# Attention layers on one core: the output projection as seven half products over two halves of an image, with its weight sums kept in DRAM, one pool of half tiles, and residuals added on GpSimd

## The chip, the cores and the metric

The kernel runs on one core of a Trainium2 chip. The core has five engines that run their own instruction streams and wait for each other through semaphores: TensorE (PE in the profile, its weight loads PEld), VectorE (DVE), ScalarE (ACT), GpSimd (POOL) and SyncE (SP), whose queue here issues nearly all DMAs. The metric is the time on the device in microseconds (us); lower is better. Everything is computed in float32.

## The reference

Two layers over four images of 32 x 32 positions and 768 channels. Each layer normalises its input in 32 groups of channels, does self-attention with 12 heads of 64 channels and a position bias in both directions, projects, and adds its input:

```python
qkv = x @ Wqkv
...
rel_h = jnp.einsum('bhwc,hkc->bhwk', r_q, Rh)
rel_w = jnp.einsum('bhwc,wkc->bhwk', r_q, Rw)
...
scores = scale * jnp.einsum('bqc,bkc->bqk', q, k) + bias
attn = jax.nn.softmax(scores, axis=-1)
out = jnp.einsum('bqk,bkc->bqc', attn, v)
...
return out @ Wproj + bproj
...
x = x + _L0_conv_ref(_gn(x), ...)
x = x + _L1_conv_ref(_gn(x), ...)
```

The second layer has other weights, biases on q, k and v, and another scale of the bias. An image has S = 1024 positions, so the output projection is a product of 768 x 768 weights with 768 x 1024 values for each of eight layer-images.

## The kernel before, in words

The eight layer-images ("images" from here, 0 to 7; 4 to 7 are the second layer) are worked one after the other. An image has six pairs of heads; a pair has eight units, each of 128 query positions for both heads. So there are 48 pairs and 384 units, and the loop over units (`for at, (g, n) in enumerate(units)`) writes out by hand the order of all engines' work. Channels lie on partitions, 128 at a time, as six chunks c, and the 1024 positions are two halves of 512.

In the iteration of a unit, GpSimd makes the bias tiles `sc` of the unit two ahead (`biases`, L535: two tensors of 128 x 1024), TensorE makes the scores of the next unit (L549), VectorE adds them to the bias and finds the row extremes (L561), ScalarE takes exponentials (L565), VectorE the reciprocal (L573), ScalarE or, in two of eight units, GpSimd divides one of the two heads (L579, L577). VectorE then transposes the present unit's tiles in blocks of 32 into `tb` (L585); SP stores `tb` to DRAM (`td`, L587) and one to three units later reads it back in the transposed order (`pt`, L596). At the end of units 6 and 2 `weigh` multiplies the values with the probabilities of the first and the second half of a pair (L614). `sc` has six buffers (three units), `tb` two, `td` five, `pt` two (a quarter of a pair each).

Between these come pieces of matmuls for other pairs. The projections of q, k and v (`products`, `values`) already work on sums of weights and of halves of x, seven products instead of eight. A function `crossed` (L356) runs a group of 12 matmuls of 64 contraction rows in two halves of six; the second half uses the other rows for each output. A `Crossed` object issues one half at each call; a table `same` says in which unit which half goes: the output groups O0 and O1 go in unit 5 (O0), unit 7 (O0, O1) and unit 0 of the next pair ("O1 previous"), between a first q group (G0) and a first v group (V0).

The output projection itself is done directly: for each of six output chunks o, three input chunks at a time (p = 0 in pairs 3 to 5 of the same image, p = 1 in pairs 0 to 2 of the next), `project_out_two` gives both halves. `put_result` adds the residual and the bias on VectorE (L711), SP stores this partial sum to DRAM and reads it back for p = 1 (L713), whose result is stored. In the last image the second part has no next image: groups of single matmuls (L693, contraction over 128 rows) are held in `todo` and taken in the last pair, some in each unit as `shares` says, the rest after the loop.

The next image's x is loaded in halves. Images 1 to 3 load one half early in the pair 0 for its statistics, and then again for use; GpSimd makes sums of halves in pairs 4 and 5. The group norm of the next image (`norm`) gathers means through DRAM in units 1 to 7 of pair 3 with four small DMAs, and ScalarE applies it in pair 4.

What waits for a free buffer waits on the engine or the queue that writes it first; SP's queue keeps its order, so what stands behind a waiting DMA waits too.

## Time and profile before

| | |
|---|---|
| median of three runs | 3295.09 us (3294.67 to 3298.21) |
| the profiled execution | 3297.59 us, its span 3295.9 |
| granted TensorE clock | 0.999 |
| TensorE matmul, weight loads | 99%, 57% of the span |
| VectorE, ScalarE, GpSimd | 78%, 61%, 74% |
| DMA | 1047.33 MB, mean 318 GB/s |
| output groups oo, L356 | x2112 records, mean 589 ns |
| bias tiles, L535 | x768, mean 2555 ns |

A matmul instruction of float32 leaves two records, so 2112 are 88 groups of 12. Matmuls on the two row halves overlap, so a record's mean is longer than what it adds to the engine's time; in the chain of work, which lists pieces in order of time with their start, length and engine, a piece's length is what it adds. In the table of stretches each engine's busy time is followed by its number of instructions; after the engines come the granted clock, the busy share of the 16 DMA engines and the rate in GB/s. Square brackets behind an instruction are the idle time before it and who ended it.

### The profile page before, as it was taken

What the parts mean: (1) busy time and instruction counts of PE and PEld (TensorE: products, weight loads), DVE (VectorE), ACT (ScalarE), POOL (GpSimd) and SP (SyncE); (2) the same over time, 40 slices, a digit from 0 to 9 for tenths busy, and PEclk for the clock granted to TensorE, in tenths of its full rate; (3) what the DMA queues carried; (4) which work ended last, traced back from release to release, by engine and by line L of the source; (5) the groups of instructions that cost most, each with busy time, mean ns of one, the idle gap of its engine ahead of it and who ended that gap; (6) DMA issues with size and microseconds to landing.
All of it is one profiled execution on the core that took longest, in us unless ns stands there. A gap on an engine that the chain in (4) does not pass through costs nothing.

```text
span 3295.9 us, 64321 instructions
## 1 busy us (share of the span) xinstructions
PE 3269.2 (99%) x25076; PEld 1880.4 (57%) x25076; DVE 2559.5 (78%) x4087; ACT 2002.4 (61%) x3004; POOL 2437.8 (74%) x1249
## 2 busy tenths in 40 slices
PE   8999999999999999999999999999999999999998
PEld 5565555555565555555565555655555555655554
DVE  7887778877787777787778877777777777777775
ACT  5676656666556665656656666555756566565653
POOL 7877967679677786777867778677786777777762
PEclk9999999999999999999999999999999999999999
DMA  5999899999999998999889999898998989898887
GB/s 182 331 337 328 319 330 329 320 332 319 327 337 315 333 323 304 338 322 329 316 313 335 317 330 319 314 330 315 337 320 312 324 315 341 312 319 310 318 287 272
DMA packets 395152, 1047.33 MB, mean 318 GB/s; under 512 B 34656, under 2 KB 60768, under 8 KB 345696
## 3 DMA queue, kind: packets, MB, share of 16 engines
q1 hardware_dynamic: 379296, 1015.79, 87.2%
q10 hardware_dynamic: 15552, 27.43, 2.2%
q8 instruction: 198, 3.24, 0.4%
q14 instruction: 106, 0.87, 0.1%
HBM read 568.00 MB, written 475.09 MB: 316 GB/s over the span
## 4 chain that ended last, share of the span: by engine, by line
PE 96%; DMA 2%; DVE 1%; issue 0%; ACT 0%; POOL 0%; SPq 0%; DVEq 0%; POOLq 0%; ACTq 0%
PE pj L356 22%; PE av L614 20%; PE s L549 20%; PE oo L356 14%; PE pv L356 11%; PE pj L384 4%; PE tp L487 2%; PE pv L441 2%; DMA td<-tb 1%; PE o L693 1%; DVE tb L585 1%; DMA xn<-in_x 0%; DMA pt<-td 0%; DVE sc L561 0%; DVE s L325 0%
## 5 line engine op out<-in xcount | busy, mean ns | idle before, releaser
L535 POOL TENSOR_TENSOR sc<-rel 128x1024 f32<-128x1024 f32 x768 | 1937.9, 2555 | 426.9 <-DVE tb L585 406.8
L561 DVE CUSTOM_DVE_ANT_0 sc<-s,sc 128x1024 f32<-128x1024 f32 x768 | 911.3, 1223 | 363.9 <-PE s L549 316.2
L579 ACT ACTIVATE sc<-sc,sm 128x1024 f32<-128x1024 f32 x674 | 743.5, 1144 | 613.1 <-DVE sm L573 461.0
L565 ACT ACTIVATE sc<-sc,sm 128x1024 f32<-128x1024 f32 x768 | 878.7, 1146 | 360.4 <-DVE sm L561 357.8
L585 DVE STREAM_TRANSPOSE tb<-sc 128x1024 f32<-128x1024 f32 x768 | 908.5, 1224 | 13.5 <-DMA td<-tb 12.7
L549 PE MATMUL s<-k,q 64*128 64x512 f32 x3072 | 738.1, 596 | 1.9 <-DVE sm L561 1.4
L614 PE MATMUL av<-pt,v 128*64 128x256 f32 x6144 | 686.4, 381 | 5.6 <-DMA pt<-td 4.0
L614 PEld LDWEIGHTS av<-pt,v 128*64 128x64 f32 x6144 | 435.1, 137 | 286.4 <-issue 40.5
L356 PE MATMUL oo<-attn,wo 64*128 64x512 f32 x2112 | 475.3, 589 | 0.0
L549 PEld LDWEIGHTS s<-k,q 64*128 64x128 f32 x3072 | 284.4, 187 | 300.3 <-issue 267.4
L577 POOL TENSOR_SCALAR sc<-sc,sm 128x1024 f32<-128x1024 f32 x94 | 105.7, 1124 | 351.4 <-DVE sm L573 351.4
L356 PEld LDWEIGHTS oo<-attn,wo 64*128 64x128 f32 x2112 | 200.9, 187 | 228.0 <-issue 227.0
L356 PEld LDWEIGHTS pv<-wv,xn 64*128 64x128 f32 x4608 | 270.8, 188 | 35.0 <-issue 25.6
L356 PE MATMUL pv<-wv,xn 64*128 64x128 f32 x4608 | 273.2, 272 | 0.6 <-DVE wv L345 0.6
L356 PE MATMUL pj<-xn,wa 64*128 64x512 f32 x1152 | 264.3, 590 | 1.6 <-DVE xn L253 1.0
L356 PE MATMUL pj<-xn,w 64*128 64x512 f32 x1152 | 263.2, 589 | 0.0
L356 PE MATMUL pj<-s,wc 64*128 64x512 f32 x576 | 262.6, 589 | 0.0
L356 PE MATMUL pj<-s,w 64*128 64x512 f32 x576 | 262.6, 589 | 0.0
L356 PEld LDWEIGHTS pj<-xn,w 64*128 64x128 f32 x1152 | 111.7, 187 | 135.5 <-issue 133.8
L356 PEld LDWEIGHTS pj<-xn,wa 64*128 64x128 f32 x1152 | 111.6, 187 | 135.6 <-issue 123.6
L458 DVE TENSOR_TENSOR v<-pv,v 128x512 f32<-128x512 f32 x216 | 140.2, 686 | 57.4 <-ACT v L460 42.4
L510 ACT COPY rel<-raw 32x256 f32<-32x256 f32 x384 | 154.9, 403 | 3.6
(102 smaller groups left out, 2656.4 us busy)
## 6 DMA issues: line engine op xcount, KB each, us to landing
td<-tb SPq DMA_DIRECT2D x384, 1024.0 KB, 5.4
pt<-td SPq DMA_DIRECT2D x382, 1024.0 KB, 8.6
tdr<-t ACTq DMA_DIRECT2D x96, 256.0 KB, 5.4
part<-res SPq DMA_DIRECT2D x84, 256.0 KB, 4.2
res<-part SPq DMA_DIRECT2D x84, 256.0 KB, 4.7
wa<-in_wqk SPq DMA_DIRECT2D x48, 384.0 KB, 3.9
wc<-in_wqk SPq DMA_DIRECT2D x48, 384.0 KB, 5.3
wv<-in_wv SPq DMA_DIRECT2D x24, 768.0 KB, 11.2
```

The source lines that it names most:

```text
L356: nc.tensor.matmul(to, lhsT=w, rhs=x, start=at == half == 0, stop=at == 0 and half == 1)
L384: nc.tensor.matmul(t[:, h, :], lhsT=w[rows, c, :], rhs=x[c][rows, :], start=(c == 0), stop=(c == NB - 1),)
L458: add = lambda to, x, y: nc.vector.tensor_tensor(to, x, y, ALU.add)
L510: nc.scalar.copy(rel[rows], raw[rows, :, :, WIDE - 1 - HW - y : WIDE - 1 - y])
L535: nc.gpsimd.tensor_tensor(sc.rearrange("p (a k) (u l) -> p a (k u) l", a=4, l=8), rel[:, h, m, :].unsqueeze(1).unsqueeze(3).to_broadcast(s ...
L549: nc.tensor.matmul(ps[h][:, cols], lhsT=q[rows, n * P : (n + 1) * P], rhs=k[rows, cols], start=True, stop=True,)
L561: nc.vector.tensor_tensor_reduce(out=sc, in0=ps[h], in1=sc, scale=-scale, scalar=BIG, op0=ALU.add, op1=ALU.min, accum_out=st[:, 0, h : h + 1],
L565: nc.scalar.activation(sc, sc, AF.Exp, bias=st[:, 0, h : h + 1], scale=-1.0, accum_out=st[:, 1, h : h + 1],)
L577: nc.gpsimd.tensor_scalar(sc, sc, st[:, 2, h : h + 1], 1.0, ALU.mult, ALU.mult)
L579: nc.scalar.mul(sc, sc, st[:, 2, h : h + 1])
L585: nc.vector.transpose(tb[:, :, h, :], sc_of[g, n, h])
L614: nc.tensor.matmul(av[rows, at * 2 * P : (at + 1) * 2 * P], lhsT=v_of[g][:, k, rows], rhs=pt_of[g, quarter].rearrange("p n r k h i -> p (n ...
```

## The change

The output projection of images 0 to 6 is now done from all six chunks at once, as seven half products. Write the weights as four blocks of three chunks by three and the attention as two chunk groups by two position halves. For each o in 0 to 2 (chunks o and o + 3 of the output) there are four groups: a, b and c are crossed groups of two products each, d an uncrossed group of six matmuls with one product. The groups go in pairs 4 and 5 (a) of the image and 0 to 3 (b, c, d) of the next. Parts of the result are held in half tiles (`kept_x`, `kept_y`) and finished on VectorE.

- The sums of weight blocks are made once, by GpSimd in image 0 (units 8 to 28: `combined`, four loads, four subtractions and four stores for each of six layer and o combinations), kept in DRAM and loaded like the weights.
- The sums of attention halves are made by GpSimd (`out_sums`, 12 per image, in pairs 4, 5, and 0 and 2 of the next).
- The residual is loaded a unit after a result is there, added by GpSimd in the unit after that, and stored in the next (`complete`). Partial sums no longer go through DRAM.
- `xn`, attention, residuals and partial results are half tiles of one pool with 35 buffers; v has three buffers instead of four, output weights four instead of two.
- x of the next image is loaded whole at the start of pair 4 (six halves in unit 0, three each in units 1 and 2); for images 1 to 3 twelve halves are loaded in pairs 0 to 3 for the statistics alone.
- Group norm works on chip: VectorE transposes blocks of 32, sums over groups, squares on GpSimd, in units 6 and 7 of pair 3 and unit 0 of pair 4.
- In the last image only two output groups are done early instead of four; eight pieces of p = 0 instead of four are in `todo`, and `shares` grows from 18 to 33 matmuls.

```diff
+UNITS = 35
...
-    xpool = ctx.enter_context(tc.tile_pool(name="x", bufs=3 * NC))
-    apool = ctx.enter_context(tc.tile_pool(name="attn", bufs=6))
+    upool = ctx.enter_context(tc.tile_pool(name="unit", bufs=UNITS))
-    vpool = ctx.enter_context(tc.tile_pool(name="v", bufs=4))
+    vpool = ctx.enter_context(tc.tile_pool(name="v", bufs=3))
-    iopool = ctx.enter_context(tc.tile_pool(name="io", bufs=4))
...
+        def spread(to, x):
+            total = work[:, : HW // n]
+            nc.vector.tensor_reduce(total, by_group(x), mybir.AxisListType.X, ALU.add)
+            nc.vector.tensor_scalar(
+                by_group(to), total.unsqueeze(2).to_broadcast([P, HW // n, n]), 1.0 / n, None, ALU.mult
+            )
+        def group_means():
+            nc.vector.tensor_copy(w0[:, :2], means[:, im, :])
+            nc.vector.transpose(w1, w0)
+            spread(w0, w1)
...
+    def combined(l, o, stage, held={}):
+        if stage == 0:
+            tables[l, o] = dram.tile([4, P, NB * P], FP, tag=f"tw{l}_{o}", name=f"tw_{l}_{o}")
+            held[l, o] = [unit(f"t{k}_{l}_{o}")[:, : NB * P] for k in range(4)]
+            for k, t in enumerate(held[l, o]):
+                nc.sync.dma_start(
+                    out=t, in_=a[f"wo{l}"][o + k % 2 * NB][:, k // 2 * NB * P : (k // 2 + 1) * NB * P]
+                )
+            return
+        b11, b12, b21, b22 = held[l, o]
+        sub = lambda to, x, y: nc.gpsimd.tensor_tensor(to, x, y, ALU.subtract)
+        if stage == 1:
+            sub(b11, b12, b11)
+            sub(b12, b22, b12)
+        elif stage == 2:
+            sub(b22, b22, b11)
+            sub(b21, b21, b22)
+        else:
+            for k, t in enumerate((b11, b22, b12, b21)):
+                nc.sync.dma_start(out=tables[l, o][k], in_=t)
...
+    def out_product(im, kind, o):
...
+        if kind == "d":
+            for c in range(NB):
+                for h, rows in enumerate(ROWS):
+                    nc.tensor.matmul(
+                        t[:, h, :], lhsT=ws[0][rows, c, :], rhs=half(1, 0)[c][rows],
+                        start=(c == 0), stop=(c == NB - 1),
+                    )
+        else:
+            xs = {
+                "a": lambda: (half(0, 0), [s3_of[im, c] for c in range(NB)]),
+                "b": lambda: (half(1, 0), half(0, 0)),
+                "c": lambda: (half(0, 1), half(1, 1)),
+            }[kind]()
+            yield from crossed(t, range(NB), lambda t, c, h, rows: (
+                t[:, h, :], ws[h][rows, c, :], xs[h][c][rows]
+            ))
...
+        if kind == "a":
+            kept_x[o], kept_y[o] = unit(f"ox_{im}_{o}"), unit(f"oy_{im}_{o}")
+            nc.scalar.copy(kept_x[o], t0)
+            add(kept_y[o], t1, kept_x[o])
+        elif kind == "b":
+            x, y, r = kept_x[o], kept_y[o], unit(f"or_{im}_{o}_0")
+            with_bias(r, t0, x, o)
+            add(x, t1, x)
+            add(y, t1, y)
+            complete(im, o, 0, r)
...
+    def complete(im, o, i, r, delay=1):
+        l, b = images[im]
+        def load():
+            res = unit(f"res_{im}_{o}_{i}")
+            load_half(res, l, b, o, i)
+            at_sums.setdefault(here[0] + 1, []).append(lambda: add(res))
+        def add(res):
+            nc.gpsimd.tensor_tensor(res, res, r, ALU.add)
+            at_start.setdefault(here[0] + 1, []).append(lambda: store(res))
...
+    out_plan = {
+        0: ("b0", "b1", None), 1: ("b2", "c0", None), 2: ("c1", "d0", "d1"), 3: ("c2", "d2", ""),
+        4: ("a0", "", ""), 5: ("a1", "a2", None),
+    }
...
+    streams = [(0, n) for n in range(6)] + [(1, 3), (1, 4), (2, 4), (2, 5), (3, 3), (3, 4)]
...
+    out_sum_steps = {
+        (4, 0): (0, 3, 0), (4, 1): (0, 3, 1), (4, 2): (0, 3, 2), (5, 2): (0, 1, 0), (5, 4): (0, 1, 1),
+        (0, 3): (1, 1, 2), (0, 1): (1, 2, 0), (0, 2): (1, 2, 1), (0, 4): (1, 2, 2),
+    }
+    combining = {}
+    for k in range(LAYERS * NB):
+        for stage in range(4):
+            combining.setdefault(NT + 4 * k + stage + (stage > 0), []).append((k // NB, k % NB, stage))
...
-                    todo = put_out(im, 0, range(8, 12)) + put_out(im, 1, range(12))
+                    todo = put_out(0, range(4, 12)) + put_out(1, range(12))
-            shares = [0, 3, 0, 4, 4, 3, 0, 4]
+            shares = [3, 6, 0, 6, 6, 6, 0, 6]
```

## The prediction

> **What bounds the kernel now.** I read the engine totals first, then the chain that ended last, then stretches of about one pair of heads each, and last the queues of the two runners-up, DMA and GpSimd.
>
> ```profile
> PE 3269.2 (99%) x25076; PEld 1880.4 (57%) x25076; DVE 2559.5 (78%) x4087; ACT 2002.4 (61%) x3004; POOL 2437.8 (74%) x1249
> ...
> PE 96%; DMA 2%; DVE 1%; issue 0%; ACT 0%; POOL 0%; SPq 0%; DVEq 0%; POOLq 0%; ACTq 0%
> ```
>
> TensorE is busy 99% of the span and is 96% of the chain; every other engine has at least a fifth of the time free. The stretches below are pairs 1, 2, 3 and 4 of the first image, then pairs 3, 4 and 5 of the fourth, roughly, then the end of the last pair.
>
> ```profile
> core 0: us, PE busy (x) PEld busy (x) DVE busy (x) ACT busy (x) POOL busy (x), PEclk, DMA share, GB/s
> 93.00:154.00 61.00, 58.52 (x456) 34.90 (x456) 49.91 (x80) 39.57 (x60) 50.45 (x26) 0.97 0.94 344
> 154.00:214.00 60.00, 59.42 (x504) 36.26 (x502) 51.96 (x86) 39.42 (x60) 46.56 (x22) 1.00 0.91 318
> 214.00:273.00 59.00, 58.56 (x466) 33.88 (x462) 50.14 (x84) 42.47 (x63) 50.45 (x26) 1.00 0.91 329
> 273.00:342.00 69.00, 69.00 (x550) 41.12 (x549) 53.83 (x84) 46.55 (x70) 51.44 (x26) 1.00 0.94 336
> 1427.00:1493.00 66.00, 66.00 (x500) 37.41 (x498) 53.23 (x92) 42.24 (x63) 48.80 (x26) 1.00 0.91 318
> 1493.00:1562.00 69.00, 69.00 (x550) 40.26 (x548) 53.48 (x86) 46.59 (x71) 51.78 (x27) 1.00 0.95 336
> 1562.00:1628.00 66.00, 66.00 (x500) 37.37 (x498) 49.75 (x78) 41.47 (x62) 60.33 (x35) 1.00 0.90 319
> 3202.00:3257.00 55.00, 49.71 (x234) 23.39 (x232) 43.21 (x65) 33.72 (x45) 30.21 (x12) 1.00 0.93 324
> ```
>
> In the middle TensorE has no gap at all, so every matmul taken out there should shorten the run until something else is late. The next thing is near: DMA is at 0.90 to 0.95. Where it was full, it moved this much:
>
> ```profile
> 280.00:300.00 20.00, 20.00 (x143) 11.05 (x144) 14.14 (x23) 12.16 (x20) 13.59 (x7) 1.00 1.00 352
> 320.00:340.00 20.00, 20.00 (x114) 9.78 (x113) 17.57 (x30) 14.80 (x22) 16.29 (x9) 1.00 0.98 356
> ```
>
> So I take 354 GB/s as its ceiling. From the chain in order of time come the prices on TensorE: one half of a crossed group (12 records) is 2.58, a group without crossing (pj L384, six matmuls) also 2.58, and the single matmuls at the end 21.45/24 = 0.89 each.
>
> ```profile
> 258.73 2.58 PE pj L384 x12
> ...
> 268.17 2.58 PE oo L356 x12
> ...
> 3257.19 21.45 PE o L693 x48
> ```
>
> GpSimd's slack in pair 4 of the fourth image is what it waits before its three divisions, after which it must do the sums of the next image:
>
> ```profile
> 1528.41 1.12 POOL L577 TENSOR_SCALAR sc<-sc,sm 128x1024 f32<-128x1024 f32 x1 [6.25 <-DVE sm L573]
> ...
> 1545.36 1.12 POOL L577 TENSOR_SCALAR sc<-sc,sm 128x1024 f32<-128x1024 f32 x1 [3.72 <-DVE sm L573]
> ...
> 1597.95 1.12 POOL L577 TENSOR_SCALAR sc<-sc,sm 128x1024 f32<-128x1024 f32 x1 [5.12 <-DVE sm L573]
> ```
>
> [...] VectorE's own sum of two SBUF tiles took 1214 ns (s, L325), the same size with one PSUM operand 686 (v, L458). All new VectorE additions take one operand from PSUM[...].
>
> **The change, part by part.**
> *Seven half products.* Images 0 to 6 had 12 crossed groups each of 2 x 2.58 = 5.16. Now they have nine and three uncrossed ones of 2.58: 3 x 2.58 = 7.7 less per image, lying in pair 4 unit 0, pair 4 unit 7 and pair 5 unit 0. But the groups also move. Image 0's pairs 3 to 5 held six groups and now hold three (a0, a1, a2 in pairs 4 and 5): -15.5. Images 1 to 6: -7.7 x 6 = -46.4. Image 7's stretch had ten groups (six for image 6, four of its own) and gets six crossed, three uncrossed and two of its own: -2.6; the two groups it no longer does early become 12 single matmuls in the last pair, 12 x 0.89 = +10.7. Together -53.8 of TensorE time.
>
> *Bytes.* Summed over the program's DMAs, 1043.1 MB becomes 1025.4: the partial sums (22.0 written, 22.0 read) and group norm's small round trips go; three more weight loads per output chunk pair and the table come (24 loads and 24 stores of 0.197 for the table). But the table is made in image 0, units 8 to 28, and streams and residuals are spread anew. In pairs 1, 2, 3 of image 0 the bytes go from 19.4, 19.4, 18.9 to 22.0, 22.8, 23.6 MB: 68.4 MB, at 354 GB/s 193 us. TensorE's work there is 58.5 + 59.4 + (58.6 - 2.6 for the half group that goes) = 174. DMA becomes the bound for these three pairs and is 19 us short. Part of it is taken up by the distance between a probability tile's store and its use (its read is issued nearly three units before the weighting that needs it; landing took 8.6 in the median), and VectorE may not write a third tile before the first of two has been stored. I take 15 us of stall; the bounds are 5 (more can lag than I think) and 24 (GpSimd's 8 us of table subtractions per pair, raising it to about 59 us a pair, add to it). What is late there is the td store, so the transposes, so the next scores.
>
> *Pair 4 of images 1 to 6.* GpSimd gets 12 residual additions and 12 sums per image at 1.28 (row L325). Counted by unit, pair 4 rises from 60.2 to 67.8 us, while TensorE gives it 62 to 64. Of its waits above, 6.25 loses 1.3 to a new sum and 2.6 to the matmuls that go, and is still a wait; 3.72 meets 6.4 us of new work in units 1 and 2 and is overrun by 2.7; 5.12 loses that and two halves of 2.58 and is overrun by 2.7. Behind the last division stand that unit's transposes on VectorE, behind these the next scores' release; VectorE has a wait of about 1.7 us on TensorE's scores in most units there (1.66 before several L561 in order of time). DMA in pairs 3 and 4 carries 45.2 to 45.7 MB = 128 to 129 us against 135.5 - 5.2 = 130.3: full but not over. Six x halves now come in one burst at unit 0 and are normalised on ScalarE a unit later. I charge 1 us per image, +6; bounds 0 and 24 (4 each).
>
> *The last pair.* Of the +10.7, part fits into gaps: TensorE was idle 55.00 - 49.71 = 5.3 us there. Against it, this pair's bytes rise by 1.4 MB (4 us) for residuals fetched later. I take -2, bounds -5 and +4.
>
> *Nothing.* Group norm by transposes is a dozen small VectorE instructions of about 0.2, hidden by its 316 us of waits for scores; uncovered it would cost 2 us an image. VectorE's result additions go from 24 of 0.72 per image to 27 (+2 us per image), ScalarE gets three copies of 0.58, under the same cover; uncovered 4 us an image. v with three buffers: the tile reused in unit 3 was last read by the weighting of unit 2, earlier on the same TensorE. The half-tile pool is filled to its last buffer; some loads on SP follow a GpSimd addition or TensorE group of the unit just ended. SP already waits up to 11.1 us at once (td behind wa, L345) without a TensorE gap, so a few us more of it are free; uncovered, see the last rival.
>
> Sum: -53.8 + 15 + 6 - 2 = -34.8. The profiled execution took 3297.6 (span 3295.9), so 3262.8; it lies 2.5 above the median shown, 3295.1, so I say 3260.
>
> **Rivals.**
> *All of it arrives.* DMA lags without stopping anyone and GpSimd catches up: 5 instead of 15, 0 instead of 6, -5: -53.8 + 5 - 5 = -54, 3241. For it: DMA held 350 GB/s in 280 to 340 with TensorE full. Against it: three pairs in a row at 22 to 24 MB in 58 us are more than any stretch before.
> *Pairs 4 and 5 take it back.* GpSimd and the x burst cost 4 us in each of six images, image 0 stalls 20: -53.8 + 20 + 24 - 1 = -11, 3284. For it: the two overruns of 2.7 above. Against: VectorE's cover.
> *Slower: SP's queue.* Loads into half tiles wait on SP for their readers, td stores stand behind them, and VectorE's two tb buffers hold up the softmax. At 2 us for each of the 42 pairs after the first image it costs 84 and ends at 3345; it decides against the change from 35/42 = 0.8 us per pair. For it: the pool has no free tile in places. Against: each such wait is for work of the unit just ended, 3 to 5 us, with nearly a unit (8.5) until the next store.
>
> **How the numbers follow.** The forecast case has 0.48 (its own range 3248 to 3274), all of it 0.20, taken back 0.21, SP 0.11. The range 3240 to 3289 leaves out the slower rival, about half of the first rival's lower side and the upper part of the second. About 0.2% (6.6 us) is what a measurement can tell: faster is below 3288.5. The first two cases and most of the third are faster: 0.48 + 0.20 + 0.14 = 0.82; same 0.07 from the third; slower 0.11.
>
> **What would show it.** Right: out-product groups fall to 7/8 in the chain; pairs in the middle of an image keep 66.4 and 69.1 us of full TensorE; per image about 7 us less; in the first image, pairs 1 to 3 take 62 to 66 us at a DMA share near 1.0 with TensorE waiting for td or pt; GpSimd's idle before L577's successor almost vanishes in pair 4. Wrong: TensorE gaps in every pair behind td stores (SP's queue), scores waiting for GpSimd's bias tiles in pairs 4 and 5 by several us, or a first image without gaps.

## The result and the profile after

The changed kernel takes 3402.91 us (median of four runs, 3399.25 to 3403.85) against 3295.76 for the kernel before on the same chip: 1.032 times as long, interval 1.0304 to 1.034. The forecast was 3260, with a range of 3240 to 3289 and 0.11 for slower. It was wrong in sign, and the loss is larger than in the rival that ended slower (3345).

The totals of the engines and the chain of work that ended last, of the changed kernel:

```profile
PE 3268.4 (96%) x24800; PEld 1893.0 (56%) x24800; DVE 2559.6 (75%) x4064; ACT 2013.1 (59%) x3025; POOL 2668.4 (79%) x1458
...
PE 70%; DMA 11%; POOL 7%; DVE 6%; issue 3%; ACT 2%; SPq 1%; ACTq 0%; DVEq 0%; POOLq 0%
```

TensorE has 276 records fewer, as it should, yet its busy time hardly changes (3269.2 before). So it works more slowly somewhere, and it now stands idle for 129 us of the span instead of 27. It was 96% of the chain and is 70%: transfers, GpSimd and VectorE have taken the rest. GpSimd has 230.6 us more to do. The granted clock is 0.990 (0.999 before), and the span is 3397.5 against 3295.9.

Next the stretches. The first image, pairs 1 to 3, and the end of the last pair; columns as in the table of before (busy time and instructions of each engine, granted clock, DMA share, GB/s):

```profile
core 0: us, PE busy (x) PEld busy (x) DVE busy (x) ACT busy (x) POOL busy (x), PEclk, DMA share, GB/s
94.00:156.00 62.00, 60.54 (x479) 35.67 (x480) 51.41 (x81) 39.89 (x61) 53.28 (x29) 1.00 0.96 345
156.00:217.00 61.00, 56.60 (x475) 34.51 (x473) 45.91 (x73) 38.91 (x59) 52.80 (x32) 1.00 0.95 340
217.00:276.00 59.00, 52.69 (x426) 32.03 (x424) 43.18 (x67) 35.74 (x56) 47.89 (x29) 0.97 0.98 357
...
3280.00:3340.00 60.00, 54.08 (x247) 24.31 (x244) 40.10 (x61) 33.07 (x48) 35.58 (x15) 0.94 0.90 314
```

And four stretches in the fifth image, cut at the starts of the weightings (av) in units 2 and 6: from unit 6 of pair 2 to unit 2 of pair 3, on to unit 6, to unit 2 of pair 4, to unit 6.

```profile
core 0: us, PE busy (x) PEld busy (x) DVE busy (x) ACT busy (x) POOL busy (x), PEclk, DMA share, GB/s
1885.00:1926.20 41.20, 36.47 (x286) 21.45 (x284) 24.78 (x41) 22.30 (x34) 21.52 (x10) 0.92 0.78 274
1926.20:1959.90 33.70, 32.71 (x218) 17.65 (x216) 29.74 (x46) 17.86 (x26) 31.26 (x19) 1.00 0.75 259
1959.90:1996.60 36.70, 34.78 (x322) 21.82 (x320) 30.58 (x54) 25.18 (x37) 26.46 (x16) 1.00 0.96 346
1996.60:2031.80 35.20, 33.43 (x220) 19.35 (x218) 28.23 (x44) 23.71 (x37) 32.63 (x20) 1.00 0.98 357
```

The reader should see two kinds of loss. In the first of the four, TensorE loses 4.7 us and the clock falls to 0.92, while DMA is only 0.78 busy and GpSimd half: something is asked for too late. In the others the clock is full, and TensorE loses one or two microseconds while DMA (0.96 and 0.98) or GpSimd (31.26 of 33.70, 32.63 of 35.20) is nearly full.

The expectations below name such a stretch by the pair in which it begins: *Xa* runs from the weighting in unit 6 of pair X to that in unit 2 of the next pair, *Xb* from there to unit 6. Here are their lengths in the sixth image (image 5), which loads no half tiles ahead for statistics; the starts of the av matmuls are taken from each run's trace. "Work left" is the stretch before, less 2.58 for each half group that went (one in 3a, two in 4a).

| run | 2a | 2b | 3a | 3b | 4a | 4b | 5a |
|---|---|---|---|---|---|---|---|
| before | 34.1 | 32.3 | 36.8 | 32.3 | 34.1 | 32.3 | 36.8 |
| work left | 34.1 | 32.3 | 34.2 | 32.3 | 28.9 | 32.3 | 36.8 |
| the change | 41.3 | 33.3 | 36.5 | 35.1 | 30.9 | 32.3 | 38.3 |
| d1early | 34.1 | 33.3 | 36.6 | 36.7 | 30.9 | 32.3 | 38.3 |
| burst | 40.8 | 33.3 | 36.4 | 32.6 | 30.9 | 32.3 | 38.3 |
| evac | 34.1 | 33.3 | 36.8 | 32.6 | 29.0 | 34.1 | 36.8 |
| lean | 34.1 | 33.3 | 35.0 | 32.6 | 29.1 | 34.0 | 36.8 |
| no_adds | 34.1 | 32.3 | 34.3 | 32.3 | 29.0 | 32.6 | 36.8 |
| best1 | 34.1 | 33.3 | 34.5 | 33.8 | 29.0 | 34.1 | 36.8 |
| onvec | 35.9 | 32.3 | 36.0 | 32.3 | 29.0 | 34.0 | 36.8 |
| slots_streams | 34.1 | 32.3 | 35.8 | 32.5 | 31.3 | 34.2 | 36.8 |
| pair3 | 34.1 | 32.3 | 35.1 | 33.9 | 29.0 | 34.0 | 36.8 |

What TensorE itself waited for in the changed kernel, four rows of its list of waits (sum in us, times, longest):

```profile
PE od L702 <- DMA wo_d<-in_wo: 33.6, 7, 5.4
...
PE pj L355 <- DVE wa L344: 12.9, 10, 1.7
...
PE pj L355 <- DVE oy L716: 6.8, 7, 1.0
PE o L812 <- DMA wo<-in_wo: 5.9, 2, 5.5
```

The first is once in each of seven images. In order of time in the fifth image, first from the chain, then TensorE's own timeline with the idle time in brackets:

```profile
1902.87 0.93 SPq L109
...
1903.84 5.12 DMA wo_d<-in_wo
```

```profile
1909.10 4.94 PE L702 MATMUL od<-attn,wo_d 64*128 64x512 f32 x12 [4.73 <-DMA wo_d<-in_wo]
```

The weights of group d1 go out on SP's queue at 1903.84, behind the loads of residuals (L109), and land at 1908.96; the product that needs them could have begun at 1904.4, when the scores ahead of it ended. Their request stands in `fetch_out`, which each group calls at its end for the group two places later (`k = order_of[im, kind, o] + 2`). Two places after c1 is d1. But c1 and d0 end together in unit 7 of pair 2, so d1 comes in the very next unit, the one in which its weights are requested. After the wait, twelve records that take 2.74 in the same timeline elsewhere take 4.94.

### The profile page after: what moved, and what is told of

It reads as the page before. It is cut to its first block, busy times and chain, and to the rows that moved or that the text cites. A ratio compares the mean times of both kernels' runs of the same rounds, so it can differ in the third digit from the quotient of the medians.

```text
span 3397.5 us, 63925 instructions
## 1 busy us (share of the span) xinstructions
PE 3268.4 (96%) x24800; PEld 1893.0 (56%) x24800; DVE 2559.6 (75%) x4064; ACT 2013.1 (59%) x3025; POOL 2668.4 (79%) x1458
## 4 chain that ended last, share of the span: by engine, by line
PE 70%; DMA 11%; POOL 7%; DVE 6%; issue 3%; ACT 2%; SPq 1%; ACTq 0%; DVEq 0%; POOLq 0%
PE pj L355 17%; PE s L548 15%; PE av L613 15%; PE pv L355 8%; DMA td<-tb 5%; POOL sc L534 4%; PE ob L355 3%; PE pj L383 3%; PE oc L355 2%; DVE tb L584 2%; PE tp L486 2%; PE oa L355 2%; DMA rel<-tdr 2%; PE od L702 1%; PE pv L439 1%
## 5 line engine op out<-in xcount | busy, mean ns | idle before, releaser
L548 PE MATMUL s<-k,q 64*128 64x512 f32 x3072 | 746.2, 597 | 2.7 <-DVE sm L560 2.2
L613 PE MATMUL av<-pt,v 128*64 128x256 f32 x6144 | 690.0, 382 | 17.9 <-DMA pt<-td 17.8
L548 PEld LDWEIGHTS s<-k,q 64*128 64x128 f32 x3072 | 295.9, 187 | 297.2 <-issue 258.5
L355 PE MATMUL pj<-xn_False,wa 64*128 64x512 f32 x1008 | 232.3, 593 | 22.5 <-DVE wa L344 11.5
L355 PE MATMUL pj<-xn_True,w 64*128 64x512 f32 x1008 | 235.1, 598 | 10.7 <-DVE k L399 10.7
L355 PEld LDWEIGHTS pj<-xn_False,wa 64*128 64x128 f32 x1008 | 96.7, 188 | 148.9 <-issue 98.9
L509 ACT COPY rel<-raw 32x256 f32<-32x256 f32 x384 | 154.8, 403 | 39.5 <-DMA rel<-tdr 35.9
L355 PEld LDWEIGHTS pj<-xn_True,w 64*128 64x128 f32 x1008 | 102.3, 189 | 130.2 <-issue 127.0
L355 PEld LDWEIGHTS pv<-wv,s 64*128 64x128 f32 x2304 | 137.0, 188 | 26.2 <-issue 21.6
L491 ACT COPY t<-tp 128x512 f32<-128x512 f32 x96 | 56.1, 585 | 150.3 <-PE tp L486 150.2
L564 ACT ACTIVATION_READ_ACCUMULATOR sc<-sc,sm 128x1 f32 x768 | 144.3, 188 | 0.0
L355 PEld LDWEIGHTS pj<-s,wc 64*128 64x128 f32 x576 | 104.4, 187 | 68.9 <-issue 49.4
```

What stands on the lines that cost most here:

```text
L355: nc.tensor.matmul(to, lhsT=w, rhs=x, start=at == half == 0, stop=at == 0 and half == 1)
L509: nc.scalar.copy(rel[rows], raw[rows, :, :, WIDE - 1 - HW - y : WIDE - 1 - y])
L548: nc.tensor.matmul(ps[h][:, cols], lhsT=q[rows, n * P : (n + 1) * P], rhs=k[rows, cols], start=True, stop=True,)
L564: nc.scalar.activation(sc, sc, AF.Exp, bias=st[:, 0, h : h + 1], scale=-1.0, accum_out=st[:, 1, h : h + 1],)
L613: nc.tensor.matmul(av[rows, at * 2 * P : (at + 1) * 2 * P], lhsT=v_of[g][:, k, rows], rhs=pt_of[g, quarter].rearrange("p n r k h i -> p (n ...
```

## The experiments

Each edit is one against the changed kernel (later ones against the run named), and times are medians, with the ratio to the kernel before on the same chip and its interval.

**d1early: one request earlier.** After c0 the weights of d0 and d1 are both requested.

```diff
-        early.append(lambda: fetch_out(k))
+        if (kind, o) == ("c", 0):
+            early.append(lambda: (fetch_out(k), fetch_out(k + 1)))
+        elif (kind, o) != ("c", 1):
+            early.append(lambda: fetch_out(k))
```

> The changed kernel, with the weights of d1 loaded together with those of d0, one pair earlier than its use instead of in the same unit. Theory A (a weight load that is asked for in the unit that uses it leaves TensorE without work, and TensorE's clock is then halved for some us): the seven waits of 4.8 us go (33.6) and the half clock behind them (seven times 1.7 to 3.4), so 45 to 60 us less than the changed kernel, about 3350. Theory B (GpSimd, the x burst and DMA in pairs 3 and 4 set the time, this wait only uses up the same slack): at most 15 less, 3388 or more.

Measured: 3353.39 us (3350.43 to 3358.35), ratio 1.0178 [1.0163, 1.0193], 49.5 below the changed kernel. The wait is gone and 2a is back at 34.1. The row of the group's matmuls, of the changed kernel and of this run (records, busy us, mean ns, idle before):

```profile
L702 PE MATMUL od<-attn,wo_d 64*128 64x512 f32 x252 | 73.4, 724 | 33.6 <-DMA wo_d<-in_wo 33.6
```

```profile
L702 PE MATMUL od<-attn,wo_d 64*128 64x512 f32 x252 | 57.6, 589 | 0.0
```

The wait itself was 33.6. TensorE's busy time falls by another 12.9 (3268.4 to 3255.5): these matmuls alone by 15.8, since their mean of 724 ns becomes 589, while the rest of the program is 2.9 longer in this trace. Together that is 46.5 of the 49.5. The theory of the late weights holds; its rival, under 15 less, does not. But the run is still 57.6 above the kernel before, so this is not the only fault.

**before_late: the same fault alone, in the kernel before.** At the start of pair 3 of images 1 to 7 one 64 KB block of output weights is loaded again, ahead of the half group that reads it.

```diff
+            if (pair, n) == (3, 0) and im:
+                src = a[f"wo{images[im - 1][0]}"][NC - 1][:, (NC - 1) * P :]
+                nc.sync.dma_start(out=wo_of[im - 1, NC - 1, NC - 1], in_=src)
```

> The kernel before, with one thing added: in unit 0 of pair 3 of images 1 to 7 a 64 KB piece of the weights of O1 is loaded a second time, in front of the half group that reads it in the same unit (the result is the same). Theory A: a gap of 4 to 5 us on TensorE in each of seven images and a half clock behind each: 40 to 60 us slower than before, and the granted clock falls from 0.999 to about 0.99. A rival where a gap costs its own length only: 28 to 35 slower, clock unchanged. Theory B, where the softmax has slack to make up for it: under 15 slower.

Measured: 3332.2 us (3330.2 to 3339.07), ratio 1.0116 [1.0101, 1.0131]: 36.4 above the kernel before, between the two expected ranges. Seven waits gave 27.2 us of idle time, and TensorE's busy time grew by 9.3 (3269.2 to 3278.5): 36.5. The granted clock is 0.997 (0.999 before). So the extra cost of the clock is real, but smaller than I had said, and the trace tells why. Two of the seven, from TensorE's timeline:

```profile
1873.30 4.54 PE L356 MATMUL oo<-attn,wo 64*128 64x512 f32 x12 [4.99 <-DMA wo<-in_wo]
```

```profile
2694.67 2.85 PE L356 MATMUL oo<-attn,wo 64*128 64x512 f32 x12 [3.53 <-DMA wo<-in_wo]
```

In images 1 to 4 the gaps were 4.46, 4.36, 4.26 and 4.99 and the half group after each took 4.5 to 5.1; in images 5 to 7 they were 2.70, 3.53 and 2.93 and it took 2.85. The stretch 2a grew by 6.3 to 7.0 in the first four and by 3.0 to 3.8 in the others. The clock records of the changed kernel show half clock behind such gaps: after its first 60 us it sets in 13 times and lasts 3.41 us (six times) or 6.83 (seven), and all 13 starts lie a whole number of 3.41 us apart. Cut into windows of 3.41 us at these points, all ten of that trace at full clock in which TensorE was idle for more than 2.05 us were followed by half clock, none of the 938 with less than 1.75 was, and three of the seven between were. One of the three held a single gap of 1.77 (TensorE's busy time, then the clock):

```profile
core 0: us, PE busy (x), PEclk, DMA share, GB/s
1182.90:1186.31 3.41, 1.64 (x8) 1.00 0.89 266
1186.31:1189.72 3.41, 3.41 (x10) 0.50 1.04 425
```

In the same trace a gap of 2.42 at 1126.96 that such a point cut into 1.32 and 1.10 met no half clock. All nine gaps above 3.6 after the first 60 us of the changed kernel (4.37 to 5.49), the seven waits for d1's weights among them (4.65 to 5.36), were followed by half clock. I had not asked this in the prediction, where a microsecond of waiting was priced at a microsecond.

**tables: the weight sums spread.** Layer 0's three sums eight units apart in pairs 1 to 3 of image 0, layer 1's at the start of pair 5 of images 0 to 2.

```diff
-            combining.setdefault(NT + 4 * k + stage + (stage > 0), []).append((k // NB, k % NB, stage))
+            at = NT + 8 * k if k < NB else (k - NB) * NP * NT + 5 * NT
+            combining.setdefault(at + stage + (stage > 0), []).append((k // NB, k % NB, stage))
```

> The changed kernel, with the sums of output weights spread: layer 0's three at every eighth unit of pairs 1 to 3 of image 0, layer 1's three in pair 5 of images 0, 1 and 2. Theory (DMA and GpSimd work of the tables makes the first image 27 us longer than its matmuls): 12 to 20 less than the changed kernel, 3383 to 3391. Rival (the first image is late for another reason, such as the rest of the start): within 4 of 3403.

Measured: 3397.87 us (3393.68 to 3400.14), ratio 1.0314 [1.0296, 1.0331], 5.0 below the changed kernel: a miss. In image 0, 0b to 3b together fall from 236.0 to 224.6, so 11.4 is gained there. But in pair 5, 4b and 5a grow from 32.3 and 38.3 to 34.1 and 40.1 in images 0 and 1, and to 34.1 and 39.1 in image 2: 9.8 of it is paid back. I had taken pair 5 to have room for two subtractions in a unit, beside the loads and stores of the sums. It has not.

**burst: first halves two at a time.** In the changed kernel, SP gets six loads of first halves at the start of pair 4; here two each at units 5 and 6 of pair 3 and at unit 0 of pair 4.

```diff
-            if pair == 4 and n < 3 and not end:
-                for c in range(NC) if n == 0 else range(3 * n - 3, 3 * n):
-                    load_x(im + 1, c, n > 0)
+            if (pair, n) in ((3, 5), (3, 6), (4, 0)) and not end:
+                for c in {5: (0, 1), 6: (2, 3), 0: (4, 5)}[n]:
+                    load_x(im + 1, c, 0)
+            if pair == 4 and n in (1, 2) and not end:
+                for c in range(3 * n - 3, 3 * n):
+                    load_x(im + 1, c, 1)
```

> The changed kernel, with the first halves of the next x loaded two at a time in units 5 and 6 of pair 3 and unit 0 of pair 4, instead of six in unit 0 of pair 4. Theory C (the burst stands in SP's queue ahead of the pair's shifted position terms, GpSimd waits for these, and so the scores): from unit 6 of pair 3 to unit 2 of pair 5 each image loses 7 us, most of which comes back: 20 to 40 less, 3363 to 3383. Rival (GpSimd's own added work causes it): less than 8 less.

Measured: 3381.06 us (3375.71 to 3383.34), ratio 1.0258 [1.0243, 1.0273], 21.9 below. In images 1 to 6 3b goes from 35.1-36.7 to 32.6-33.4. What the burst did is seen on SP's queue and on GpSimd in the fifth image; the changed kernel, then SP's queue in this run:

```profile
1993.28 8.21 SPq L519 DMA_DIRECT2D rel<-tdr  x4
```

```profile
2005.13 5.04 POOL L534 TENSOR_TENSOR sc<-rel 128x1024 f32<-128x1024 f32 x2 [2.49 <-DMA rel<-tdr]
```

```profile
1983.84 8.68 SPq L519 DMA_DIRECT2D rel<-tdr  x4
```

These four small transfers bring back the position terms. In the changed kernel SP starts to issue them 3.4 us before the weighting of unit 2, here 5.8 us before it, since only two of the six loads still stand ahead. With the burst GpSimd waited 2.49 for them before the biases, behind which stand VectorE's scores and the next k; here it waits 0.45. What the burst does not explain is how long their issue takes: 8.21 us with it and 8.68 without, where the kernel before needs 1.94. Why is not shown, and it stays so in best1 (8.73).

**evac: the copy on VectorE.** The edits of d1early and burst, and the first copy of an a group made on VectorE.

```diff
-            nc.scalar.copy(kept_x[o], t0)
+            nc.vector.tensor_copy(kept_x[o], t0)
```

> The changed kernel with three edits: d1's weights asked for one group earlier, the next image's first halves loaded two at a time, and the copy of the first half of an a group's result made by VectorE in place of ScalarE. The first two alone gave -49.5 and -21.9 us, so if they add up they give 3331.5. Theory: the wait of VectorE's sum oy on ScalarE's copy ox (64.7 us in all in the changed kernel, queued behind ScalarE's copies of the positions) is what lengthens the stretches 4a and 5a by 2.0 and 1.5 us in each of images 0 to 6, so 4a falls from 30.9 to 28.9-29.3, 5a from 38.3 to 36.8-37.2, and the time to 3300-3315. Rival: those stretches are long because GpSimd is late with the biases, whoever copies: 4a and 5a stay, and the time is 3325-3338.

Measured: 3321.85 us (3311.92 to 3322.55), ratio 1.0072 [1.0057, 1.0087]. If the first two edits add up to 3331.5, which was not run by itself, this is 9.6 less; 16 to 31 was expected, and the rival had at most 6. 4a fell to 29.0 and 5a to 36.8, the work left to within 0.1, so the copy was the cause there. But 4b, which had been clean, grew from 32.3 to 34.1. The wait had moved on, as the waits of TensorE show; the changed kernel, then this run:

```profile
PE pj L355 <- DVE wc L344: 5.2, 7, 1.0
```

```profile
PE pj L355 <- DVE wc L344: 8.3, 15, 1.0
```

The wait for oy from L716 (6.8 in the list above) is gone. A small VectorE operation (wc, L344) releases the next k group; it stands behind scores that wait for GpSimd's bias tiles. In image 5 TensorE waits 0.40 for it, and the scores just before take 2.92 in place of 1.89: 1.4 of the 1.8. I read this as GpSimd being late: with two microseconds less in 4a, it is that much later in 4b. The run no_adds, further down, bears this out: with less work on GpSimd 4b falls to 32.6-32.9 in images 1 to 6.

**lean: no blocked multiplication in the norm.** The reduction itself writes the group sum to each member; the factor goes to two small GpSimd operations, and the three scratch tiles change roles accordingly.

```diff
-            total = work[:, : HW // n]
-            nc.vector.tensor_reduce(total, by_group(x), mybir.AxisListType.X, ALU.add)
-            nc.vector.tensor_scalar(
-                by_group(to), total.unsqueeze(2).to_broadcast([P, HW // n, n]), 1.0 / n, None, ALU.mult
-            )
+            nc.vector.tensor_reduce(
+                by_group(to), by_group(x).unsqueeze(2).to_broadcast([P, HW // n, n, n]),
+                mybir.AxisListType.X, ALU.add,
+            )
...
+            nc.gpsimd.tensor_scalar(w0, w0, 1.0 / n, None, ALU.mult)
             nc.gpsimd.tensor_tensor(w1, w1, w0, ALU.subtract)
             nc.gpsimd.tensor_tensor(w1, w1, w1, ALU.mult)
+            nc.gpsimd.tensor_scalar(w1, w1, 1.0 / n, None, ALU.mult)
```

> The same three edits, and the group means of the norm spread by the reduction itself (its input broadcast), without the VectorE multiplication from SBUF to SBUF that took up to 2.56 us beside a GpSimd addition; the factor goes to two small GpSimd operations. Theory: that blocked multiplication holds VectorE's queue and with it the stretch 3a (35.2-36.8 us where 34.2 is the work): 3a falls to 34.2-35 and the time lies 7-17 us below the run without this edit. Rival: 3a is long because the groups c2 and d2 end there and leave six VectorE sums: 3a stays, and the times agree within 3 us.

Measured: 3312.87 us (3308.71 to 3315.16), ratio 1.0049 [1.0033, 1.0066], 9.0 below evac; 3a falls from 36.8 to 35.0 in image 5. The operation at fault, in the timeline of the changed kernel, and the reduction that takes its place, as a group in this run (mean 283 ns):

```profile
1971.94 2.56 DVE L278 TENSOR_SCALAR turned<-nrm 128x32 f32<-128x32 f32 x1
```

```profile
L276 DVE TENSOR_REDUCE turned<-turned 128x32 f32<-128x128 f32 x14 | 4.0, 283 | 0.2
```

The multiplication's median was 181 ns, but in 3 of 14 cases, one each in images 4 to 6, it took 2.52 to 2.56 us, which is the length of one GpSimd bias operation (2.55). In the changed kernel each of the three began within 0.07 us after such an operation had begun and ended within 0.05 us of its end. In evac three multiplications took 2.25 to 2.59, while here all 14 reductions take 278 to 287 ns. But this explains only a part of the gain. In images 4 to 6, where the multiplication took 2.25 to 2.59, 3a is 2.5, 1.8 and 1.3 shorter than in evac, 5.6 of the 9.0; in images 1 to 3, where it took 181 ns in evac too, it is 2.4, 1.0 and 0.6 shorter, for a reason that is not shown. In the prediction I had looked at VectorE's sums of two SBUF tiles alone, and not at these new small operations. (The 1214 ns given there is a mean, too: of the six sums three took 678 to 679 ns and three 1739 to 1755.)

**no_adds: GpSimd without the residual additions.** Against evac; the residual is loaded and stored, without the projection.

```diff
-            nc.gpsimd.tensor_tensor(res, res, r, ALU.add)
```

> The run with three edits (weights of d1, first halves, copy on VectorE), with GpSimd's addition of the residual left out: the residual is loaded and stored as it is, so the output lacks the projection. Theory: the 84 additions on GpSimd make its biases late, which costs 1.3 us in the stretch 2b and part of 3a and 3b in each of images 1 to 7: the time lies 10-25 us below the run with the three edits, 2b is 32.3. Rival: 2b waits for weights that land late, not for GpSimd: 2b stays at 33.3-33.7 and the time within 4 us.

Measured: 3281.05 us (3279.17 to 3284.08), ratio 0.9956 [0.9941, 0.9971], 40.8 below evac: the theory's direction, but well over its size. 2b is 32.3, and 3a is 34.3 although the norm is that of the change: it was 36.8 in evac and 35.0 with the norm's edit. In this run the multiplication is blocked in images 1 and 2 alone (1.60 and 2.29), and there 3a is 35.4 and 36.1. VectorE's wait for bias tiles, in evac and here:

```profile
DVE sc L560 <- POOL sc L534: 126.3, 112, 2.7
```

```profile
DVE sc L560 <- POOL sc L534: 74.2, 64, 2.7
```

**best1: sums spread more finely, last weights earlier.** Against lean: layer 0's sums as in tables; layer 1's in pair 5 of images 1 to 3, with one subtraction in a unit instead of two; and the last image's output weights one chunk further ahead.

```diff
+            if k < NB:
+                combining.setdefault(NT + 8 * k + stage + (stage > 0), []).append((k // NB, k % NB, stage))
+    for o in range(NB):
+        for at, stage in zip((43, 45, 46, 47, 48, 49), (0, 4, 5, 7, 8, 9)):
+            combining.setdefault((o + 1) * NP * NT + at, []).append((1, o, stage))
...
-                fetch(3)
+                fetch(5)
...
-            fetch(2 * o + 5)
+            fetch(2 * o + 7)
```

> The four edits (weights of d1, first halves, copy on VectorE, norm without the blocked multiplication), with layer 0's weight sums eight units apart and layer 1's in pair 5 of images 1 to 3 with one GpSimd subtraction to a unit, and the last image's output weights fetched one chunk further ahead. Theory: image 0 gains some 11 us as it did with the sums spread before, pair 5 now loses under 1 us a time instead of 3.6, and the last pair loses its waits for weights (5.9 us and a stretch of half clock): 15-25 us below the run with four edits, 3265-3290 in all, under the 3295.8 of the kernel before. Rival: the sums cost the same wherever they stand, and the last pair waits for its residuals instead: within 6 us of the run with four edits.

Measured: 3291.1 us (3286.02 to 3294.36, 20 runs), ratio 0.9982 [0.9976, 0.9989], 21.8 below lean, as expected. In the traces, 0b to 3b of image 0 fall from 238.2 to 222.5, pair 5 does not grow (4b 34.0-34.1 in both), and 4a to 5a of the last image fall from 104.3 to 95.6, since its wait for weights is gone.

**onvec and onvec2: the additions on VectorE.** Against best1. The residual is loaded a unit before its group ends; result, bias and kept half are summed in place in PSUM, and a second VectorE operation adds the residual. onvec loads two first halves at unit 5 of pair 3 and four at the start of pair 4, onvec2 keeps 2, 2 and 2.

```diff
-            with_bias(r, t0, x, o)
+            with_bias(t0, t0, x, o)
...
+        res = residual[im, o, i]
+        nc.vector.tensor_tensor(res, r, res, ALU.add)
```

> The best run so far (3291.1 us: weights of d1, first halves, copy on VectorE, norm, sums spread, last weights ahead) with the residual additions taken from GpSimd to VectorE: the residual is loaded a unit before its group ends, the sum of result, bias and kept half is written over the result in PSUM, and a second VectorE operation adds the residual from there (one operand in SBUF only). First halves: two at unit 5 of pair 3, four at the start of pair 4. Theory: leaving the additions out gave -40.8 us because GpSimd's 84 additions of 1.27 us make its biases late, and with them VectorE's queue, in which the small reductions stand that release TensorE; VectorE has room for 84 more operations of 0.7 us, so 2b falls from 33.3-33.7 to 32.3-32.6, 4b from 34.1 to 33-33.5, and the time to 3262-3280. Rival: VectorE is as near its limit as GpSimd, and its sums hold the groups' PSUM or wait for the residuals landing: the stretches 0b to 3a grow by 1-3 us an image and the time is 3290 or more.

> The same with the first halves two at units 5 and 6 of pair 3 and two at the start of pair 4; the pool of half tiles is then asked for 37 of its 35 buffers in units 6 and 7 of pair 3. Theory (the burst of loads counts more than the full pool): 3b lies 0.5-1 us below that of the run with four at the start of pair 4, the time 3-7 us below. Rival (the full pool holds SyncE's queue): 3a and 3b grow by 1-4 us an image, the time is 5-20 us above.

Measured: 3338.4 us (ratio 1.0132 [1.0115, 1.015]) and 3337.47 us (1.0128 [1.0109, 1.0146]): the rival of the first, and no difference between the two. 2b and in onvec 3b are clean (32.3), as the theory had it. But in images 1 to 7 1a rose to 39.0-41.4 (36.9-37.4 in best1), in images 1 to 6 1b to 34-37 (32.3), 2a by 1.8 to 3.0 in all seven, and 3a in images 3 to 7 by 1.4 to 2.7. TensorE waits for the additions now; in this version the result stays in PSUM until the second operation has read it (onvec):

```profile
PE pj L356 <- DVE res L768: 21.1, 28, 1.3
PE pv L356 <- DVE res L768: 13.2, 14, 2.2
```

**slots and slots_streams: the additions on GpSimd, in other units.** Against best1. slots moves the additions of c1, d0, d1, c2 and d2 and the three sums for the a groups into units where GpSimd has no weights to combine. slots_streams also takes the next image's last loads out of pair 3.

```diff
+    slots = {
+        (0, 0): 9, (1, 0): 10, (2, 0): 17, (0, 1): 18, (3, 1): 18, (1, 1): 26,
+        (4, 1): 26, (3, 0): 28, (4, 0): 28, (2, 1): 34, (5, 1): 35, (5, 0): 35,
+    }
...
-        at_start.setdefault(here[0] + delay, []).append(load)
+        at_start.setdefault((im + 1) * NP * NT + slots[o, i] - 1, []).append(load)
...
-        (4, 0): (0, 3, 0), (4, 1): (0, 3, 1), (4, 2): (0, 3, 2),
+        (3, 7): (0, 3, 0), (4, 0): (0, 3, 1), (4, 2): (0, 3, 2),
```

and in slots_streams

```diff
-(2, 4), (2, 5), (3, 3), (3, 4)]
+(2, 3), (2, 4), (2, 5), (2, 6)]
```

> The best run so far (3291.1 us) with the residual additions kept on GpSimd, but those of the groups c1, d0, d1, c2 and d2 one unit later and apart from the units in which GpSimd also combines weights (units 0, 1, 3 and 5 of an odd pair): c1's two at unit 2 of pair 3, d0's and d1's at unit 4, c2's and d2's at units 2 and 3 of pair 4; and the three sums for the a groups at unit 7 of pair 3 and units 0 and 2 of pair 4 in place of 0, 1 and 2. Theory: GpSimd is not short of time on the mean but in single units (biases 5.1, weights 2 to 3, a division 1.1 and two additions 2.5 are over 10 us in a unit of about 8), and the lateness of one unit is what TensorE pays: 2b falls from 33.3-33.7 to 32.3-32.8, 4b from 34.1 to 32.3-33.5, the time to 3268-3283. Rival: GpSimd has no room left anywhere in these pairs and the lateness only moves: 2b and 4b fall, 3a or 3b grow by as much, and the time is 3286-3298.

> The same, with the last four loads of the next image's half tiles (images 0 to 2) in units 3 to 6 of pair 2 in place of units 4 and 5 of pair 2 and 3 and 4 of pair 3. Theory: the 3 to 5 us by which 3a is longer in images 1 and 2 (39.0 and 37.5 where later images have 34.4-35.1) come from these transfers, which delay the transposed weights' way through DRAM: 3a falls to 35-36.5 there, the time lies 3-8 us under the run without this edit. Rival: the transfers only move and lengthen 2a and 2b instead: within 3 us.

Measured: 3317.03 us (ratio 1.0066 [1.0051, 1.0082]), above both ranges; and 3288.12 us (0.9976 [0.9966, 0.9985]), 28.9 below the first where 3 to 8 was expected. 2b is 32.3 in images 3 to 7 of slots, as the theory said. In images 1 and 2, however, 2b is 39.7 and 40.3 and 3a 44.3 and 43.5. The additions hold their half tiles a unit longer, so with the next image's loads in pair 3 the pool would, by my count, need 36 of its 35 buffers, and a load then waits at the head of SP's queue. SP's longest waits of that kind, in slots and in slots_streams, and in slots what TensorE waits for behind it:

```profile
SPq L109 <- POOL res L768: 79.1, 20, 14.0
```

```profile
SPq L109 <- POOL res L768: 58.1, 18, 5.4
```

```profile
685.20 6.42 PE L614 MATMUL av<-pt,v 128*64 128x256 f32 x32 [7.37 <-DMA pt<-td]
```

In each of images 1 and 2 a wait of 14.0 us in SP's queue held the transposed probabilities back, by 7.37 and 8.02; in slots_streams, where none is above 5.4, TensorE waits for them less than 2 us at a time in these images. There 3a is 35.8 and 36.1, in the range that its theory gave. Apart from that, what 2b gained came back in 3a and 4a (in image 5 35.8 against 34.5 and 31.3 against 29.0).

**pair3 and pair3_s3: is there room anywhere?** Against slots_streams: the additions of c2 and d2 where the change has them; in pair3 the sums for the a groups too, in pair3_s3 not.

```diff
-        (4, 1): 26, (3, 0): 28, (4, 0): 28, (2, 1): 34, (5, 1): 35, (5, 0): 35,
+        (4, 1): 26, (3, 0): 28, (4, 0): 28, (2, 1): 33, (5, 1): 33, (5, 0): 34,
```

> The run of 3291.1 us with the next image's last four loads in units 3 to 6 of pair 2 and the residual additions of c1 at unit 2 and of d0 and d1 at unit 4 of pair 3; those of c2 and d2 and the sums for the a groups where the change has them. Theory (lateness in single units): 2b 32.3 in images 1 to 7, 3a 34.4-35.3, 4a 29.0, 4b 34.1: 1.0-1.4 us an image for seven and 3-5 for images 1 and 2, so 3272-3282. Rival (GpSimd has no room, lateness moves): 2b 32.3, but 3a 35.8-37 as in the last run, and 3284-3292.

> The same with the three sums for the a groups at unit 7 of pair 3 and units 0 and 2 of pair 4 in place of units 0, 1 and 2 of pair 4. Theory (lateness in single units): 4b falls from 34.1 to 32.5-33.3, nothing else moves, the time 6-12 us under the run without this edit. Rival (no room): from the last units of pair 4 to unit 4 of pair 5 GpSimd never waits, whatever stood before: 4b stays at 34.1, 4a may grow by up to 1, and the time is within 3 us or up to 6 us above.

Measured: 3287.81 us (3280.88 to 3291.18, ratio 0.997 [0.9958, 0.9981]) and 3288.73 us (0.997 [0.9959, 0.9982]). Both are in the rival's range: 2b stays clean, 3a and 3b take it back (35.1 and 33.9 in image 5), and moving the sums leaves 4b at 34.0-34.1 in all but one of images 1 to 6, while 3b grows in most of them, by up to 3.3. So single full units are not the whole of it: in each place tried in pairs 3 to 5, what one stretch gained others lost. That no order could do better is not shown. pair3 is the fastest complete version, 0.3% under the kernel before, but slots_streams and pair3_s3 lie within the spread of its runs. Its totals:

```profile
PE 3232.0 (98%) x24800; PEld 1868.0 (57%) x24800; DVE 2568.0 (78%) x4071; ACT 2003.5 (61%) x3004; POOL 2672.4 (81%) x1472
```

TensorE's busy time is now 37 below that of the kernel before, and the clock is 1.0; it stands idle for 54 us of the span instead of 27.

## Why the prediction was wrong, point by point

The matmul work does go, as said: where nothing else is late, 4a is 29.0 and 3a 34.3 (34.1 and 36.8 before). What failed are the prices of what moves with it. Measured against the span that the -53.8 alone would give, 3295.9 - 53.8 = 3242.1, the changed kernel loses 155.4 us. The edits recover 49.5 (d1's weights), 21.9 (first halves), 9.6 (copy), 9.0 (norm) and 21.8 (weight sums and last weights), 111.8 in all. The part that leads back to GpSimd's residual additions was 40.8 when they were left out of evac; it overlaps with the norm's, so the terms are not a strict sum. An estimate from the stretches says how much of the forecast hung on them: take no_adds, and put in best1's image 0 (0b to 4b, 16.4 shorter) and last pair (7.7 shorter), and 3281 becomes about 3257, close to the 3260 of the forecast. That was not run.

- *Seven half products: the step that failed.* It moved nine groups per image and counted their matmuls, but not their weight transfers. Where each group's weights are asked for, and how long before their use, was never looked at. For d1 the lead was 0, and that one order cost 49.5, nearly the whole gain. No item of the sum and no rival had it. The price too would have been too low, since half clock for 3.41 or 6.83 us followed each of these gaps. With this mended the time is 3353, still slower than before; the rest lies in the items below, above all in GpSimd.
- *Bytes.* Place and size were about right, and TensorE's long waits there were for pt, as I had said. I took 15 for pairs 1 to 3 of image 0. My stretches ended at the weighting in unit 6 of pair 3: they took 180.0 us before, 177.5 less the half group that goes, and 191.1 after, 13.6 more (11 in d1early, with the same code there, and 18 in burst; the stretch varies by some 4 us from run to run). What I had at nothing comes behind them: 3a and 3b of image 0 lost another 10.6 (36.4 for 29.1 of work, 35.6 for 32.3), since I charged pair 4 in images 1 to 6 alone. Spacing the sums out gained 11.4 from 0b to 3b in one run, so their crowding and GpSimd's part count, not the bytes alone. The ceiling of 354 GB/s was too low: the stretch from 217 to 276 ran at 357, and a whole fortieth of the span at 367 in pair3.
- *Pair 4.* I charged 1 us an image, with 4 as the upper bound. In image 5 it was 2.3 (3a), 2.8 (3b) and 2.0 (4a), and 1.5 more in 5a: 8.6. The two causes I named, the burst and GpSimd, are both there, but I weighed the burst in bytes ("full but not over"), while what it delayed were small transfers behind it in SP's queue (3b). What 4a and 5a lost went with the copies on ScalarE, which I had under "Nothing".
- *The last pair.* I took -2, with +4 as the upper bound. 4a to 5a of the last image grew from 91.2 to 104.1, 2.2 more than the 10.7 of matmuls (3.7 more in d1early). So -2 became a small loss, and late weights were the cause: with them in time best1 has 95.6, only 4.4 more than before.
- *Nothing.* The weakest part. The norm's edit gave 9.0, of which 5.6 in the images with a blocked multiplication, and the copies on ScalarE 9.6 net (3.5 an image in 4a and 5a, 1.8 of which then appeared in 4b). Both were called hidden by VectorE's 316 us of waits. But a mean share of waiting does not cover an operation that stands in the queue ahead of one that TensorE needs at that moment.
- *Slower: SP's queue.* Its mechanism is not what slowed the changed kernel: TensorE's waits for pt are 17.8 us there, in nine places, the longest three in image 0. The slots run shows that it exists, in two images, once the pool is overdrawn.
- *GpSimd.* I looked at its slack in one pair, found overruns of 2.7, and let VectorE absorb them; the +6 of pair 4 was all that the sum had for it, where leaving out the additions alone gave 40.8, mostly in 2b to 4b. The 230 us added to an engine at 74% turned out to be the largest item that no rearrangement here removed. Left open is whether a plan with fewer GpSimd operations, rather than others, would reach the forecast; and how much of the 40.8 is GpSimd's time and how much comes from the half tiles.

## What to carry to other kernels

When a group of work is moved, list with it when each of its operands is asked for, and by what count ("two groups later" is a time only as long as groups keep their distance). An engine's mean idle share covers nothing by itself: for each new operation ask what stands behind it in its queue and when TensorE needs that. A trade that takes 54 us from the bound engine and gives 230 to one at 74% needs to be checked in the fullest stretch of that engine, since there the end of one wait is the start of the next.

## What the hardware did that I had not expected

- In the changed kernel half clock set in 13 times after the first 60 us, at times a whole number of 3.41 us apart, each time for 3.41 or 6.83 us. Of the windows of 3.41 us cut at these points and at full clock, all ten with more than 2.05 us of idle TensorE were followed by it and none of the 938 with less than 1.75. One gap of 1.77 in a single window was followed by it, one of 2.42 across a border was not, and all nine above 3.6 were. After a gap of 4.26 to 5.36 a half group took 4.4 to 5.5 us instead of 2.7 to 2.9, so by my estimate (4.7 of wait, some 2.2 of slower matmuls) a wait of 4.7 us for a late transfer costs about 7.
- A 181 ns VectorE multiplication of 128 x 32 took 2.52 to 2.56 us in 3 of 14 cases beside GpSimd's bias operations; a reduction with a broadcast input spread the same sums in 278 to 287 ns in all 14 cases.
- The DMA rate over a stretch of some 82 us reached 367 GB/s, in pair3, above the 352 and 356 that I had taken for full.
